# A metaformer block with a spectral filter: combining the spectra at k and -k behind the mixing, scaling in the rectification, and taking the mean of x on TensorE

## Chip, cores and metric

The kernel runs on one core of one Trainium2 chip. The metric is the time of one execution on the device in microseconds (us), as the median of several runs. Lower is better. A change of about 0.5% (14 us) is what a measurement of this kernel can tell from none.

## What is computed

The input x has shape (8, 128, 128, 96): eight images b of 128 x 128 pixels (h, w) with 96 channels. Cut to what matters, the reference is:

```python
z     = layernorm(x)                                  # over the 96 channels
x_pre = scale * relu(z @ w1.T) ** 2 + bias            # 192 channels
xf    = rfft2(x_pre)                                  # over h and w, 128 x 65 frequencies
r     = softmax(mlp([mean(z), mean(relu(bn(z @ sp_w.T)))]))   # 3 weights for each of 192 channels
comb  = sum_s r[s] * resized(cw_s)                    # complex filter, one of three sizes resized to 128 x 65
x     = x + irfft2(xf * comb) @ w2.T
out   = x + ffn_fp8(layernorm(x))                     # 96 -> 384 -> 96, products in float8
```

## The kernel before

Each image passes three streams, which the kernel calls a, s and c.

**Stream a** (function `before`) works in 32 units u of four columns w, and in 8 blocks of 16 columns. `load_x` loads a block with h on the partitions, `measure` takes its statistics on VectorE (DVE), and `rstd` (operations `variance`, `root`, `inverse`, `rest`) turns them into 1/deviation, partly on GpSimd (POOL). `store_r` writes these 128 x 16 numbers to DRAM (`Rd`), and `load_r` reads them back, broadcast over 96 partitions (`rB`, 128 DMAs of 384 KB). `load_xT` loads the same pixels with the channels on the partitions (`zT`, 8 columns at a time, four buffers); a 97th row holds ones, so that the bias of the batch norm comes with the product. `scale` (L771) multiplies `zT` by `rB` on DVE and sums each channel beside it, which gives the mean of z. `project` (L784) multiplies by `w1` and `sp_w` at once (240 columns per image column; the subtraction of the mean is in the weights), `rectify` (L795, ScalarE, ACT) takes two image columns at a time from PSUM through relu, `square` (L802) squares them, and `context` (L809, POOL) adds up the spatial context. `transform` (L813) is the Fourier transform along h, `put` and `fold` combine the halves w and 127-w, and `store_y` writes the result to DRAM. After the last unit nine small steps `rate_v0` to `rate_n` compute the three filter weights.

**Stream s** (function `spectrum`) works on 33 groups g. A group up to 30 holds four rows of the real transform along h, that is cosine and sine at two frequencies k and k+32. `load_y` and `load_t` load them and the filter rows (from `T`, filled at the start by `rows` and `row_put`), `weigh` (L987, POOL) applies the weights, `along_w` (L997) is the transform along w, and `filters_of` (L1014) resizes the filters along w, on 52 of 64 rows, `T` having rows 52 to 63 filled with zeros by `padding`. `copy_sr`, `make` (L1037), and `times` (L1043, L1048) build the spectra at k and -k and multiply them by the filters. `turn_back` (L1059, POOL) forms real and imaginary parts of both products into `rr`, and `real_basis` (L1072, L1074, POOL) adds and subtracts those of k and -k into `xf`. For each of 16 pairs p of groups, `mix_low` and `mix` (L1108) multiply by `w2` on quarters of TensorE (64 x 64, each a product of 96 columns) into two PSUM banks `pv`; `mixed` (L1126, ACT) copies each (384 columns) to `V`, `invert` (L1130) is the inverse transform along w, `inverted` copies it, and `store_v` stores it. The last pair also holds the frequencies 0, 32 and 64, which stand alone.

**Stream c** (function `after`) takes the inverse transform along h (`last`, L1216), adds x, normalises (`measure`, `rstd`, `quantise` L1240), and runs the float8 layers: `turn8`, `first` (L1259), `accumulated` (L1266), `biased` (L1270), `hidden` (L1274), `second` (L1281), `put8`, `bias` (L1296), `add_up` (L1299, POOL), `store`.

**What sets the order.** Nothing runs in the order in which it is written. Each step is an `Op` with the steps that it needs and the PSUM banks it takes (six banks are shared; `until` names what frees one). `in_order` is a list scheduler: it plays through the five engines with a cost for each kind of step (`COST`), picks among the steps that are ready by a place (`WINDOWS` for stream and image, `OFFSETS` for the kind, `WAIT`, `PATIENCE` and `TURN` as weights), and the program is then issued in that order, fixed on every engine. DMAs of SyncE (SP) stand in one such order too; ACT issues `store_y` and `store_v`. Most buffers are two deep, so that a step waits for the step two blocks, groups or pairs earlier.

Of the kernel before, what the change touches and what calls it, by code (L numbers as in the profile page):

```python
# [34 lines left out]
F32 = mybir.dt.float32  # L35
# [33 lines left out]
    "a": ((-493.8, 43.6), (391.2, 548.2), (341.5, 669.9), (360.3, 112.8), (272.4, 474), (949.3, 682.8), (1532.2, 298.2), (2022.4, 291.1)),  # L69
    "s": ((419.4, 108), (361.2, 702.1), (621.3, 470.7), (1129.7, 501.9), (1112.5, 414.1), (1261.5, 485.3), (2142.2, 519.8), (1769.1, 212.4)),  # L70
    "c": ((643.4, 448.3), (913.9, 146.9), (1128.5, 301.3), (1948.4, 242), (1978.4, 471.2), (2323.9, 476.2), (2115.4, 99.6), (2601.6, 522.4)),
}
OFFSETS = {
    "a_context": -48.63,
    "a_fold": 49.78,
    "a_inverse": -197.71,
    "a_load_r": -12.98,
    "a_load_x": 18.54,
    "a_load_xT": -82.99,
    "a_measure": 28.7,  # L80
    "a_project": 54.76,
    "a_put": 22.3,
    "a_rate_e": -72.58,
    "a_rate_n": 307.71,
    "a_rate_p0": -87.61,
    "a_rate_p1": -45.78,
    "a_rate_p2": 8.73,
    "a_rate_v0": -246.94,
    "a_rate_v1": 95.58,
    "a_rate_v2": -255.23,  # L90
    "a_rate_v3": 112.84,
    "a_rectify": 7.95,
    "a_rest": 13.94,
    "a_root": -29.71,
    "a_scale": 65.86,
    "a_square": -3.1,
    "a_store_r": 47.62,
    "a_store_y": -73.43,
    "a_transform": -140.71,
    "a_variance": 57.57,  # L100
    "c_accumulated": -127.17,
    "c_add_up": -24.29,
    "c_bias": -7.57,
    "c_biased": -79.11,
    "c_first": -54.8,
    "c_hidden": 21.22,
    "c_inverse": 24,
    "c_last": -35.87,
    "c_load_v": -86.64,
    "c_measure": 192.55,  # L110
    "c_put8": 71.54,
    "c_quantise": 113.84,
    "c_quantise_v": 412.46,
    "c_residual": 7.8,
    "c_rest": -56.04,
    "c_root": 58.58,
    "c_second": -187.49,
    "c_store": 64.06,
    "c_turn8": -545.98,
    "c_turned8": 70.7,  # L120
    "c_variance": -102.78,
    "s_alone_t": 116.39,
    "s_alone_x": 156.62,
    "s_alone_z": 122.58,
    "s_along_w": -138.44,
    "s_copy_sr": -78.4,
    "s_filters_of": -23.17,
    "s_invert": -43.99,
    "s_inverted": -179.15,
    "s_load_t": 88.39,  # L130
    "s_load_y": 36.3,
    "s_make": 62.83,
    "s_mix": 40.57,
    "s_mix_low": -82.45,
    "s_mixed": -49.42,
    "s_real_basis": 33.95,
    "s_store_v": -18.14,
    "s_times": -182.14,
    "s_turn_back": 123.89,
    "s_weigh": -6.86,  # L140
}
WAIT, PATIENCE, TURN = (0.1, 0, 0, 0.06, 1.5), (16.9, 0.166, 10.6, 0.53, 42.4), 13.18
# [13 lines left out]
    "a_project": (PE, 0.975, 0),  # L156
    "a_transform": (PE, 0.809, 0),
    "a_rectify": (ACT, 0.57, 0),
# [4 lines left out]
    "a_scale": (DVE, 1.215, 0),  # L163
# [3 lines left out]
    "a_rest": (POOL, 1.11, 0),  # L167
# [10 lines left out]
    "s_real_basis": (POOL, 0.91, 0),  # L178
# [3 lines left out]
    "s_mixed": (ACT, 0.48, 0),  # L182
    "s_invert": (PE, 0.81, 0),
# [4 lines left out]
    "c_last": (PE, 0.809, 0),  # L188
# [14 lines left out]
    "a_rate_v0": (DVE, 0.73, 0),  # L203
    "a_rate_p0": (PE, 0.25, 0),
    "a_rate_v1": (DVE, 0.14, 0),
# [6 lines left out]
    "_make_weights": (DVE, 7.4, 0),  # L212
    "_others": (DVE, 1.5, 1),
    "_weights": (DVE, 5, 2),
    "_padding": (POOL, 1, 2),
    "_rows": (PE, 1.2, 0),
    "_row_put": (DVE, 1.25, 1),
    "_next_pool": (SP, 0, 0),
# [271 lines left out]
def metaformer_kernel(ctx: ExitStack, tc: tile.TileContext, a: dict, out: bass.AP):  # L490
# [465 lines left out]
    def spectrum(b, t0, P):  # L956
# [164 lines left out]
        def mix(p):  # L1121
            mix_part(p, (2, 3))
# [297 lines left out]
```

## Time and profile before

| | us |
|---|---|
| median of 3 runs | 2853.39 |
| lowest and highest | 2841.11, 2855.94 |
| the profiled execution | 2853.48 |
| its span in the profile | 2851.7 |
| TensorE (PE) busy | 2493.0 |
| VectorE (DVE) busy | 2273.5 |
| ScalarE (ACT) busy | 2130.2 |
| GpSimd (POOL) busy | 2062.8 |

The mean granted clock of TensorE is 0.933 of full speed, and the DMA engines moved 621.55 MB. In the profile, L12 is line 12 of the kernel; a group of instructions has a line `engine op out<-in`, the shapes, the count, its busy time, the mean of one in ns, and the idle time of its engine ahead of it with what ended it. A float32 product counts as two matmul records. Busy times of a group are those in which at least one of its instructions ran.

### The profile page before, as it was taken

How to read it: one execution, taken by the hardware profiler on the slowest of the kernel's cores; microseconds unless marked ns; L12 is line 12 of the kernel's file. 1: busy time of each engine (PE TensorE's matmuls, PEld its weight loads, DVE VectorE, ACT ScalarE, POOL GpSimd, SP SyncE). 2: the span in 40 equal slices, each digit the busy share in tenths (PEclk: the TensorE clock that was granted, in tenths of full speed). 3: DMA queues.
4: the chain of work that ended last, by engine and by line, in shares of the span. 5: the costliest groups of instructions: out<-in, count | busy, mean ns of one | idle time of the engine just before them, and what ended most of it. 6: DMA issues, size and time to landing. Idle time of an engine off the chain costs nothing. (4 is left out here: it accounts for less than half of the span.)

```text
span 2851.7 us, 98748 instructions
## 1 busy us (share of the span) xinstructions
PE 2493.0 (87%) x40122; PEld 1759.1 (62%) x40122; DVE 2273.5 (80%) x5110; ACT 2130.2 (75%) x4204; POOL 2062.8 (72%) x2983
## 2 busy tenths in 40 slices
PE   5788999899998999988989999999899888887775
PEld 3456666666766676766666666666667555665443
DVE  4567667887997899888878877897888987778785
ACT  2255544688886788978996577779799798787987
POOL 3136886777877887767888788798888787888433
PEclk9689998999999999989999999999999987989876
DMA  7688878988798898977669978785687663666431
GB/s 223 210 280 250 245 208 230 294 234 231 227 277 240 223 275 261 276 230 220 201 181 276 287 223 249 216 258 163 205 242 224 178 188 110 197 178 172 156 122 56
DMA packets 785657, 621.55 MB, mean 218 GB/s; under 512 B 578366, under 2 KB 719558, under 8 KB 785178
## 3 DMA queue, kind: packets, MB, share of 16 engines
q1 hardware_dynamic: 697138, 464.21, 58.9%
q10 hardware_dynamic: 88064, 151.02, 14.9%
q8 instruction: 316, 5.18, 0.8%
q14 instruction: 139, 1.14, 0.1%
HBM read 406.92 MB, written 208.16 MB: 216 GB/s over the span
## 5 line engine op out<-in xcount | busy, mean ns | idle before, releaser
L1059 POOL TENSOR_TENSOR rr<-t 128x390 f32<-128x390 f32 x512 | 500.6, 989 | 145.9 <-DVE t L1043 142.9
L784 PE MATMUL px<-W1S,zT 97*128 97x240 f32 x2048 | 513.8, 390 | 38.6 <-DVE yst L825 15.3
L784 PEld LDWEIGHTS px<-W1S,zT 97*128 97x128 f32 x2048 | 391.1, 199 | 137.9 <-DVE yst L825 23.8
L1266 ACT CAST y<-ph 128x512 f16<-128x512 f32 x768 | 410.9, 603 | 43.8 <-PE ph L1259 38.7
L813 PE MATMUL py<-X,F 128*128 128x384 f32 x1024 | 422.9, 530 | 16.4 <-ACT sr L1030 3.0
L795 ACT ACTIVATE rl<-px 128x480 f32<-128x480 f32 x512 | 289.9, 577 | 168.8 <-PE px L784 142.6
L1240 ACT ACTIVATE z<-t,ln_m,ln_r 128x96 fp8e5<-128x96 f32 x960 | 407.3, 476 | 10.8 <-DMA yt<-Yd 5.0
L1274 ACT ACTIVATE h<-y 128x1536 fp8e5<-128x1536 f16 x256 | 383.9, 1501 | 22.5 <-DVE y L1270 11.7
L1037 DVE TENSOR_TENSOR d<-pz,sr 128x390 f32<-128x390 f32 x512 | 265.7, 553 | 133.8 <-ACT sr L1030 132.6
L1270 DVE TENSOR_TENSOR y<-y,b1q 128x1536 f16<-128x1536 f16 x256 | 317.3, 1240 | 57.2 <-ACT y L1266 55.7
L1108 PE MATMUL pv<-w2C,xf 64*64 64x96 f32 x12288 | 319.9, 251 | 28.7 <-issue 24.0
L825 DVE TENSOR_TENSOR yst<-py,yb 128x384 f32<-128x384 f32 x512 | 261.8, 547 | 98.3 <-ACT yb L819 50.8
L809 POOL TENSOR_TENSOR sacc<-sacc,rl 128x192 f32<-128x192 f32 x248 | 167.7, 676 | 222.4 <-ACT rl L795 214.7
L1108 PEld LDWEIGHTS pv<-w2C,xf 64*64 64x64 f32 x12288 | 283.9, 138 | 71.6 <-issue 46.5
L987 POOL TENSOR_TENSOR tb<-tb,r 128x384 f32<-128x384 f32 (+1 forms) x264 | 302.0, 1145 | 27.2 <-DMA tb<-T 26.4
L1072 POOL TENSOR_TENSOR xf<-rr 128x390 f32<-128x390 f32 x256 | 291.3, 1138 | 13.6
L1043 DVE TENSOR_TENSOR t<-d,pf 128x780 f32<-128x780 f32 x256 | 245.2, 958 | 63.2 <-PE pf L1014 33.4
L1259 PE MATMUL ph<-zT,W1q 96*128 96x512 fp8e5 x768 | 258.4, 420 | 35.5 <-DVE zT L1255 20.0
L997 PEld LDWEIGHTS pz<-F,yt 64*64 64x64 f32 x12480 | 225.6, 138 | 93.6 <-issue 34.3
L997 PE MATMUL pz<-F,yt 64*64 64x65 f32 x12480 | 257.1, 226 | 20.6 <-issue 8.4
L1014 PE MATMUL pf<-RW,tb 52*64 52x130 f32 x6240 | 243.0, 283 | 31.7 <-POOL rr L1059 8.7
L1074 POOL TENSOR_TENSOR xf<-rr 128x378 f32<-128x378 f32 x256 | 266.9, 1043 | 0.0
(117 smaller groups left out, 4509.2 us busy)
## 6 DMA issues: line engine op xcount, KB each, us to landing
yt<-Yd SPq DMA_DIRECT2D x1040, 96.0 KB
Yd<-yst ACTq DMA_DIRECT2D x256, 384.0 KB
xb<-in_xw SPq DMA_DIRECT2D x64, 768.0 KB
zT<-in_xT SPq DMA_DIRECT2D x128, 384.0 KB
rB<-Rd SPq DMA_DIRECT2D x128, 384.0 KB
tb<-T SPq DMA_DIRECT2D x256, 192.0 KB
Vd<-gst ACTq DMA_DIRECT2D x128, 384.0 KB
t<-in_x SPq DMA_DIRECT2D x64, 768.0 KB
```

The costliest lines, as they stand in the source:

```text
L784: nc.tensor.matmul(px[:, i * (MED + SCTX) : (i + 1) * (MED + SCTX)], lhsT=zTs[(b * NU // 2 + u // 2) % NZT][:, QW * (u % 2) + i0 + i, :], ...
L795: nc.scalar.activation(kept["rl", u][:, i0 : i0 + 2, :].rearrange("h w m -> h (w m)"), kept.pop(("px", u, i0)), AF.Relu)
L813: nc.tensor.matmul(py, lhsT=F1, rhs=kept["X", u][:, i0 : i0 + 2, :].rearrange("h w m -> h (w m)"), start=True, stop=True)
L987: nc.gpsimd.tensor_tensor(kept["tb", g][p, :], kept["tb", g][p, :], rates[b][p, :], ALU.mult)
L997: nc.tensor.matmul(halves[i][64 * k : 64 * k + 64, c * L : (c + 1) * L], lhsT=kept["yt", g][rows, cs, q, k, :], rhs=F2[rows, cs, :], start ...
L1059: nc.gpsimd.tensor_tensor(out, t[:, :, 0, :], t[:, :, 1, :], ALU.add if i else ALU.subtract)
L1072: nc.gpsimd.tensor_tensor(xf[:, :, :, 0:L], two(g, 0, 2, 0, L), two(g, 1, 2, 0, L), ALU.add)
L1108: nc.tensor.matmul(kept["pv", p, r][half, i * C : (i + 1) * C], lhsT=kept["xf", g][rows, cs, q, half], rhs=w2C[rows, q, :], start=(i == 0 ...
L1240: nc.scalar.activation(z, t, AF.Identity, bias=m, scale=r, saturate=False)
L1266: nc.scalar.copy(kept["y", u][:, n, :], kept.pop(("ph", u, n)))
L1270: nc.vector.tensor_tensor(y, y, b1q, ALU.add)
L1274: nc.scalar.activation(kept["h8", u], kept["y", u], AF.Relu, saturate=False)
```

## The change

Three things are done, and the order is made anew.

1. *Spectra.* `turn_back` writes real and imaginary parts of the products at k and -k straight into `xf`; `real_basis` and `rr` are gone. `mix` multiplies these by `w2` (and `w2N`, its negative, for one quarter), `mixed` copies only the half of -k from PSUM to `B` (192 columns), and a new step `combine` on DVE forms sum and difference of k and -k, 4 times a pair, reading one operand from PSUM. `invert` uses `GL` for the sums and a second matrix `GM` for the differences. The rows of `GK` are ordered to match. The columns at the two real frequencies of the half transform are now made in the filters (`ends`, `end_put`, twelve more rows of `T`, in place of the zeros), so that `filters_of` contracts over all 64 rows.
2. *1/deviation.* `scale`, `store_r`, `load_r` and `rB` are gone. `project` works on the unscaled `zT`; `rectify` multiplies by 1/deviation as it takes relu, as a per-partition scale, and so one image column at a time. The 97th row of `zT` holds the deviation instead of ones: `rest` computes it with two more small operations on POOL, `store_s` writes it to DRAM transposed (elements of 4 bytes), and `put_s` loads it as one row.
3. *Mean of z.* `gsum` multiplies x by 1/deviation on TensorE, 16 products a block, each of 32 equal columns of weights and 96 columns of x, on four strips of 32 columns of the array; `gadd` adds the blocks on DVE, and `rate_p0` and `rate_v1` finish.

Besides, `load_x` has three buffers instead of two, `invert` and `mix_low` wait for the pair two earlier instead of one, and `WINDOWS`, `OFFSETS`, `WAIT`, `PATIENCE`, `TURN` and some of `COST` have new values. The core of the diff:

```diff
-WAIT, PATIENCE, TURN = (0.1, 0, 0, 0.06, 1.5), (16.9, 0.166, 10.6, 0.53, 42.4), 13.18
+WAIT, PATIENCE, TURN = (0.07, 0.06, 0, 0.09, 2.83), (18.8, 8.11, 4.79, 4.13, 60), 1.3
...
-    "a_rectify": (ACT, 0.57, 0),
+    "a_rectify": (ACT, 0.615, 0),
+    "a_gsum": (PE, 0.9, 0),
+    "a_gadd": (DVE, 0.25, 0),
+    "a_put_s": (SP, 0.48, 0.2),
+    "a_store_s": (SP, 0.55, 2.2),
...
-        def scale(hb):
-            z = zTs[(b * NU // 2 + hb) % NZT][:C, :, :]
-            nc.vector.scalar_tensor_tensor(z, z, 1.0, kept["rB", hb], ALU.mult, ALU.mult,
-                accum_out=kept["gacc"][:, hb : hb + 1])
+        def store_s(blk):
+            t = kept["Sd", blk] = dram.tile([WB, H], F32, name="Sd", tag="Sd")
+            with nc.allow_non_contiguous_dma("deviations by columns"):
+                nc.sync.dma_start(out=t.rearrange("w h -> h w"), in_=kept["sd", blk])
+        def put_s(hb):
+            z = zTs[(b * NU // 2 + hb) % NZT][C : C + 1, :, :]
+            f = slice((hb % 2) * HB, (hb % 2) * HB + HB)
+            nc.sync.dma_start(out=z.rearrange("o w h -> o (w h)"),
+                in_=kept["Sd", hb // 2][f, :].rearrange("(o w) h -> o (w h)", o=1))
+        def gsum(blk):
+            pc = kept["pc", blk] = bank("pc")[:, :C]
+            for i in range(QW):
+                for j in range(4):
+                    w = QW * j + i
+                    nc.tensor.matmul(pc[32 * j : 32 * j + 32, :],
+                        lhsT=kept["r", blk][:, w : w + 1].to_broadcast([128, 32]),
+                        rhs=kept["x", blk][:, w, :], start=(i == 0), stop=(i == QW - 1))
...
-            nc.scalar.activation(
-                kept["rl", u][:, i0 : i0 + 2, :].rearrange("h w m -> h (w m)"), kept.pop(("px", u, i0)), AF.Relu
-            )
+            for i in range(2):
+                w = q * QW + i0 + i
+                nc.scalar.activation(kept["rl", u][:, i0 + i, :],
+                    px[:, i * (MED + SCTX) : (i + 1) * (MED + SCTX)], AF.Relu,
+                    scale=kept["r", blk][:, w : w + 1])
...
-                        p = slice(64 * s, 64 * s + R)
+                        p = slice(64 * s, 64 * s + 64)
...
+            x = kept["xf", g].rearrange("p s q n -> p (s q) n")
             if i == 0:
                 t = kept["t1", g].rearrange("p s (q c l) -> p (s q) c l", q=3, c=2)
+                nc.gpsimd.tensor_tensor(x[:, :, 0:L], t[:, :, 0, :], t[:, :, 1, :], ALU.subtract)
             else:
-                t = kept["t2", g]
-            out = kept["rr", g][:, 2 * i : 2 * i + 2].rearrange("p s q l -> p (s q) l")
-            nc.gpsimd.tensor_tensor(out, t[:, :, 0, :], t[:, :, 1, :], ALU.add if i else ALU.subtract)
-        def real_basis(g, i):
-            if i == 0:
-                nc.gpsimd.tensor_tensor(xf[:, :, :, 0:L], two(g, 0, 2, 0, L), two(g, 1, 2, 0, L), ALU.add)
-            else:
-                nc.gpsimd.tensor_tensor(xf[:, :, :, L:], two(g, 2, -1, 1, L - 2), two(g, 3, -3, 1, L - 2), ALU.subtract)
+                t = kept["t2", g][:, :, :, 1 : L - 1]
+                nc.gpsimd.tensor_tensor(x[:, :, L:], t[:, :, 0, :], t[:, :, 1, :], ALU.add)
...
         def mixed(p, r):
-            v = kept["V", p, r] = psp.tile([128, 4 * C], F32, name="V", tag="V")
-            nc.scalar.copy(v, kept.pop(("pv", p, r))[:, : 4 * C])
+            v = kept["B", p, r] = psp.tile([128, 2 * C], F32, name="B", tag=f"B{r}")
+            n = C if p == NP - 1 and r == 1 else 2 * C
+            nc.scalar.copy(v[:, :n], kept["pv", p, r][:, 2 * C : 2 * C + n])
+        def combine(p, r, cs):
+            v, a, b = kept["V", p, cs][:, r, :n], kept["pv", p, r][:, :n], kept["B", p, r][:, :n]
+            if cs == 0:
+                nc.vector.tensor_tensor(v, a, b, ALU.add)
+            else:
+                nc.vector.tensor_tensor(v, b, a, ALU.subtract)
+        def invert(p, cs):
+            pg = kept["pg", p, cs] = bank("pg")[:, : 4 * C]
+            nc.tensor.matmul(pg[:, :n], lhsT=GM if cs else GL, rhs=v[:, :n], start=True, stop=True)
...
-            at(t, mix_low, p, after=xf, banks=2, until=[one("mixed", p, r) for r in range(2)])
+            used = [[one("mixed", p, r), one("combine", p, r, 0), one("combine", p, r, 1)] for r in range(2)]
+            at(t, mix_low, p, after=xf, banks=2, until=used)
```

## Prediction

> **What bounds the kernel now.** I read the busy times first, then the same times by stage, then who TensorE waits for, then the groups that the change touches.
>
> ```profile
> PE 2493.0 (87%) x40122; PEld 1759.1 (62%) x40122; DVE 2273.5 (80%) x5110; ACT 2130.2 (75%) x4204; POOL 2062.8 (72%) x2983
> ```
>
> TensorE (PE) is the fullest, but only on average. The busy times by stretch (window, length, then PE, PEld, DVE, ACT, POOL) split at three events: the first spectral matmul (about 230 us), the last projection `px` (2204) and the last spectral matmul (2661):
>
> ```profile
> 0.00:230.00 230.00, 165.88 (x531) 107.01 (x532) 129.74 (x464) 92.33 (x167) 68.94 (x200) 0.84 0.76 237
> 230.00:2204.00 1974.00, 1821.09 (x31068) 1312.58 (x31067) 1630.33 (x3600) 1500.48 (x2985) 1558.02 (x2191) 0.97 0.82 237
> 2204.00:2661.00 457.00, 381.12 (x7707) 265.72 (x7706) 374.50 (x727) 375.61 (x766) 374.60 (x480) 0.91 0.59 169
> 2661.00:2851.00 190.00, 124.90 (x821) 73.76 (x821) 138.97 (x321) 161.75 (x288) 61.27 (x114) 0.69 0.34 111
> ```
>
> In the long stretch, 69% of the span, PE is busy 92%, and DVE (83%), POOL (79%) and ACT (76%) follow it. Only the last 190 us belong to ACT (85%). PE idles 64 + 153 + 76 + 65 = 358 us in all. The waits of PE within the long stretch (us in total, times, longest) are many and small; summed over that list by releaser they are ACT 65.8, no visible cause ("issue") 38.0, DVE 21.3, POOL 16.2, DMA 5.4:
>
> ```profile
> PE pv L1108 <- issue: 21.4, 15, 4.2
> PE pf L1014 <- POOL rr L1059: 8.3, 6, 3.6
> PE px L784 <- ACT sr L1030: 5.1, 3, 4.2
> ```
>
> So POOL, from which the change takes most, delays PE by some 16 us there; ACT delays it four times as much. The groups that the change touches, each shape apart (busy us, mean ns of one, then idle before it):
>
> ```profile
> L1059 POOL TENSOR_TENSOR rr<-t 128x390 f32<-128x390 f32 x512 | 500.6, 989 | 145.9 <-DVE t L1043 142.9 <-DVE t L1048 2.5
> L1240 ACT ACTIVATE z<-t,ln_m,ln_r 128x96 fp8e5<-128x96 f32 x960 | 407.3, 476 | 10.8 <-DMA yt<-Yd 5.0 <-POOL ln_m L729 2.5 <-DVE t L1048 1.5
> L1072 POOL TENSOR_TENSOR xf<-rr 128x390 f32<-128x390 f32 x256 | 291.3, 1138 | 13.6
> L795 ACT ACTIVATE rl<-px 128x480 f32<-128x480 f32 x512 | 289.9, 577 | 168.8 <-PE px L784 142.6 <-PE pz L997 3.6 <-DMA Yd<-yst 3.2
> L1074 POOL TENSOR_TENSOR xf<-rr 128x378 f32<-128x378 f32 x256 | 266.9, 1043 | 0.0
> L771 DVE SCALAR_TENSOR_TENSOR zT<-zT,rB 96x1024 f32<-96x1024 f32 x128 | 191.5, 1496 | 23.4 <-DMA zT<-in_xT 17.3 <-DMA rB<-Rd 3.8 <-DMA Rd<-ln_r 2.2
> L1126 ACT COPY V<-pv 128x384 f32<-128x384 f32 x256 | 111.9, 486 | 125.2 <-PE pv L1108 119.1 <-DMA yt<-Yd 2.9 <-PE py L813 2.4
> ```
>
> **What the skill says.** (1) "ScalarE: Activation LUTs", section "What ACT_TABLE_LOAD costs": an activation with immediate scale and bias takes 186 ns + 0.833 ns an element, each per-partition operand adds about 93 ns, neighbours overlap by about 93 ns. The trace agrees: by it L795 (480 wide, no such operand) is 586 ns, measured 577; L1240 (96 wide, two of them) is 452, measured 476. (2) "TensorEngine Tiling (Array Packing)", sections "Available Configurations" and "Key Properties": 128x32 gives four independent tiles, and a change of tiling mode drains the array. The trace has no 128x32 tile; it shows the drain (below). (3) "DMA: Bandwidth & Descriptors", "Rules for kernel authors": a last dimension that isn't contiguous becomes one descriptor per element. No run here shows that yet.
>
> **The change part by part**, against the profiled execution: 2853.48 us, of which the span is 2851.7, and 1.8 lie around it. The median of the runs, 2853.39, is the same.
>
> *POOL.* `real_basis` goes: 291.3 + 266.9 = 558 us. `turn_back` stays at 512 instructions, now written in the layout of `xf`: between L1059's 989 ns and the mean of L1072 and L1074 (1090), so 0 to +52; I take +30. `rest` gets two 128x16 operations for each of 64 blocks, 128 x 284 ns (L728, L729: 286 and 281) = +36. POOL falls by about 490, to 55% of the span. What it can give the end is what PE waits for it: 16 us, and some 5 more through DVE (its `y` addition, L1270, has a mean of 1240 ns against a median of 984, which I read as collisions with POOL).
>
> *DVE.* `scale` goes: 191.5, its accumulator reads 9.8, and the reduction of `gacc` 2.4: -204. `combine` adds 8 x 16 x 4 = 512 additions of 192 columns from PSUM. Nearest row: L913, a 192-wide copy from PSUM, 345 ns: +177 (bounds 262 and 519 ns, the 192-wide rows L928 and L915: 134 to 266). `gadd` adds 64 of 96 columns at some 250: +16. Net -11, from -54 to +78; DVE isn't the bound, so I count 0.
>
> *ACT.* `rectify` becomes 1024 activations of 240 columns with one per-partition scale: by (1) 479 ns each. Three `y` copies in a row take 1.60 us in the timeline where 3 x 603 are 1.81, an overlap of 0.1 each. Before 512 x (577 - 100) = 244, after 1024 x (479 - 100) = 388: +144 (+20 if the operand's 93 ns and some more hide, +195 if nothing overlaps). The kernel's own planner has 0.615 us for a pair, against 0.57 for the single one, so the new order allows for little of this. `mixed` halves to 192 columns: 256 x 486 = 124 becomes, by (1), 248 x 346 plus 24 of 96 columns at 266, 92: -32. Net ACT +112, all of it ahead of the last projection, where ACT goes from 76% to some 80%. PE's 66 us of waits for ACT grow in proportion at least (112 / 1500 of 66 = 5), and faster as slack goes: I take +10, range 5 to 30.
>
> *PE.* `gsum` adds 64 x 16 matmuls of 96 columns on 128x32 tiles. Nearest row: the mixing `pv`, also 96 columns in f32, four quarters side by side. In the chain of waits:
>
> ```profile
> 2190.23 2.01 PE pv L1108 x96
> ```
>
> That is 96 records or 48 matmuls, 12 rounds of four, 0.168 us a round. Four rounds for a block: 0.67, and 0.13 for entering and leaving: 0.8 x 64 = +51. Below: 43, if it joins a run of quarters. Above: if the four tiles don't run side by side, 16 x 0.168 x 64 = +172. Against that the new order changes less often between whole and divided array: counted in the two programs' PE order, 876 times before and 636 after. The price of one, in the PE timeline (start, length):
>
> ```profile
> 1242.06 1.52 PE L813 MATMUL py<-X,F 128*128 128x384 f32 x4
> 1243.42 0.81 PE L1216 MATMUL pk<-vin,GK 128*128 128x384 f32 x2
> 1244.16 0.93 PE L997 MATMUL pz<-F,yt 64*64 64x65 f32 x48
> 1245.02 0.42 PE L1245 MATMUL pz<-ident,z 128*96 128x128 fp8e5 x4
> ```
>
> `pk` starts 0.16 us ahead of the end of `py` (same mode), `pz` 0.07 ahead of the end of `pk`, and the next again 0.07: a change costs 0.09. 240 x 0.09 = -22. `ends` adds 12 matmuls at about 0.75 (L639's rows): +9; the split last inversion +2. The longer contraction of `filters_of` (52 to 64 rows) costs nothing, its columns being the same. Net PE +40 (32 to 160).
>
> *PSUM.* The two `pv` banks of a pair are now held until the copy and two `combine` on DVE are through, 0.35 + 2 x 0.35 instead of 0.49, plus DVE's queue; six banks serve everything. `invert` waits for all of it. Two pairs may be in flight instead of one, which covers most: +6, range 0 to 20.
>
> *DMA and SP.* 128 broadcasts of 384 KB go (50 MB of 621). The store of 8 KB a block becomes 2048 elements of 4 bytes: 131,072 packets more. Queue q1 took 58.9% for 697138 packets: 38.5 ns of one engine each, at 666 B on average. At that price they take 131072 / 16 x 38.5 ns = 315 us of all 16 engines, and 50 MB at q10's rate (151 MB in 14.9%, 355 GB/s) give back 142. Lower bound: packets for nothing. So the share of 75% moves by -5 to +6 points, from 82 to at most 91 in the long stretch: no bound. SP issues as many (64 + 128 for 64 + 128); the single `put_s` row waits behind `store_s` on it, with the loads of `yt` behind both. `project` loses the wait for a 1.5 us `scale` and gets one for a later store; the three `xb` buffers cover that. I count 0, above +40.
>
> Sum: 2853.5 + 40 - 16 - 5 + 10 + 6 = 2888; I say **2888**, 1.2% slower. The parts' own range: 2865 to 2915.
>
> **Rivals.**
> 1. *Faster: PE's idle time shrinks by more than PE's work grows.* All hinges on the 153 us of scattered idle in the long stretch: with POOL at 55% and 240 fewer changes of mode the fixed order may stall PE less. At 4% idle instead of 7.7: PE 2533, idle 65 + 80 + 141, around it 2: 2821; and the new order leaves less for the ACT-bound end (summing rows after the last `px`: ACT 599 us before, 444 after), worth up to 35: 2786. Middle 2805. It decides once idle falls from 358 below 318. For it: no single wait is large. Against: the largest releaser, ACT, gets more work.
> 2. *The array's 128x32 tiles run one after another:* 172 for 51, so 3009. The tiling page speaks against it.
> 3. *ACT or DMA takes over:* rectification at its upper bound and 4-byte packets at their price or above; PE's idle grows by 40 more: 2930. For it: nobody's price in this trace covers 4-byte runs. Against: ACT stays near 80%.
>
> **Numbers.** Forecast 0.48, rival 1 0.28, rival 2 0.04, rival 3 0.20. Within 0.5% (2839 to 2868, about what a measurement of this kernel can tell from no change) lie 0.10 of the forecast's and 0.04 of rival 1's chance. Faster 0.24, same 0.14, slower 0.62. The range reaches from rival 1's middle to beyond rival 3: 2805 to 2950; the forecast's own is 2865 to 2915.
>
> **What would show it.** Right: PE busy near 2533, ACT near 2240, POOL near 1570, DVE within 80 of before; `gsum` near 0.8 us a block; `rl` near 480 ns; idle of PE still 340 to 370, with ACT its first releaser. Wrong: PE idle under 318 (rival 1); `gsum` near 2.7 us (rival 2); DMA share over 90% with waits for `zT` or `Sd` (rival 3).

## Result, and the profile after

| | before | after |
|---|---|---|
| median of 3 runs, us | 2853.39 | 3331.29 |
| lowest and highest | 2841.11, 2855.94 | 3330.18, 3342.53 |
| span of the profiled execution | 2851.7 | 3340.7 |
| mean granted clock of TensorE | 0.933 | 0.881 |

The changed kernel takes 1.17 times as long, 95% interval 1.1635 to 1.1765. The forecast was 2888 and the range ended at 2950: neither held. The page of the changed kernel, busy times and DMA queues:

```profile
PE 2689.0 (80%) x42226; PEld 1944.4 (58%) x42226; DVE 2190.9 (66%) x5429; ACT 2211.4 (66%) x4732; POOL 1458.6 (44%) x2594
DMA packets 894834, 572.14 MB, mean 171 GB/s; under 512 B 699508, under 2 KB 840876, under 8 KB 894336
...
q1 hardware_dynamic: 806296, 414.51, 51.0%
q10 hardware_dynamic: 88064, 151.02, 18.3%
```

No engine is fuller than before. PE works 196 us longer and idles 652 us instead of 358. Queue q10 (the stores that ACT issues) carries exactly the packets of before, but they take 18.3% of 3340.7 = 611 us instead of 14.9% of 2851.7 = 425. The stretches, split at the same events (first spectral matmul, last `px`, last spectral matmul; then PE, PEld, DVE, ACT, POOL, clock, DMA share, GB/s):

```profile
0.00:270.00 270.00, 188.32 (x852) 118.88 (x856) 94.29 (x348) 101.77 (x222) 48.11 (x167) 0.81 0.75 142
270.00:2845.00 2575.00, 2124.83 (x35228) 1567.37 (x35220) 1710.87 (x4216) 1711.37 (x3729) 1177.00 (x2075) 0.90 0.74 180
2845.00:3156.00 311.00, 260.92 (x5388) 187.93 (x5386) 258.96 (x551) 246.88 (x511) 174.42 (x249) 0.90 0.56 163
3156.00:3340.70 184.70, 114.93 (x772) 70.23 (x772) 126.75 (x314) 151.34 (x272) 59.08 (x106) 0.69 0.33 109
```

All the loss lies ahead of the last `px`, where stream a runs: 2845 us instead of 2204, of which 146 come back in the third stretch because work of streams s and c has moved forward. The last two columns of the long stretch matter most: the DMA share fell (0.82 to 0.74), and so did what was moved (237 to 180 GB/s). The share says how long packets are under way, not how much arrives. The groups that the change touches:

```profile
L848 ACT ACTIVATE rl<-px,ln_r 128x240 f32<-128x240 f32 x1024 | 412.9, 480 | 247.4 <-PE px L833 151.2 <-DMA zT<-in_xT 16.8 <-DMA yt<-Yd 13.0
L1114 POOL TENSOR_TENSOR xf<-t 128x390 f32<-128x390 f32 x256 | 230.9, 902 | 626.0 <-DVE t L1100 604.8 <-PE pv L1152 14.5 <-PE ph L1332 5.6
L1185 DVE TENSOR_TENSOR V<-pv,B 128x192 f32<-128x192 f32 x248 | 87.2, 352 | 145.6 <-ACT B L1171 130.3 <-ACT V L1177 11.3 <-PE ph L1332 3.7
L1171 ACT COPY B<-pv 128x192 f32<-128x192 f32 x248 | 69.2, 329 | 205.4 <-PE pv L1152 163.1 <-remote 30.5 <-PE pz L1318 7.2
L814 PE MATMUL pc<-xb,ln_r 128*32 128x96 f32 x2048 | 76.5, 279 | 86.0 <-issue 53.8 <-POOL ln_r L556 16.8 <-ACT y L1339 9.1
```

Each operation costs about what was expected of it (furthest off is `gsum`, `pc`, with 76.5 us for 51). The time is in between them. PE's waits by releaser went from ACT 154, no visible cause 43, DVE 83, POOL 32, DMA 27 to ACT 230, no visible cause 256, DVE 70, POOL 34, DMA 40. ACT in turn waits 184 us where a DMA ended last (before: 54). On SP's own queue two waits of the new steps stand out (us in total, times, longest):

```profile
SPq L807 <- DMA Sd<-ln_s: 222.8, 38, 13.9
SPq L802 <- POOL ln_s L769: 145.8, 41, 9.8
```

L802 is `store_s`, L807 is `put_s`: the row waits for the store of 8 KB, and does so for up to 13.9 us. One such store, as the timeline shows it (start, length):

```profile
1267.88 0.38 SPq L802 DMA_DIRECT2D Sd<-ln_s  x1
...
1268.30 1.13 SPq L1035 DMA_DIRECT2D tb<-T  x1
...
1271.12 1.02 DVE L881 TENSOR_TENSOR yst<-py,yb 128x384 f32<-128x384 f32 x2 [2.07 <-PE py L869]
...
1272.20 1.08 PE L833 MATMUL px<-W1S,zT 97*128 97x240 f32 x4 [0.29 <-DVE yst L881]
...
1279.91 0.25 SPq L807 DMA_DIRECT2D zT<-Sd  x1
...
1280.71 0.52 ACTq L885 DMA_DIRECT2D Yd<-yst  x1
1281.35 0.81 ACT L848 ACTIVATE rl<-px,ln_r 128x240 f32<-128x240 f32 x2 [7.69 <-DMA tb<-T]
1282.22 1.97 PE L833 MATMUL px<-W1S,zT 97*128 97x240 f32 x4 [7.24 <-ACT rl L848]
```

and what the engines do meanwhile, in steps of 2 us (columns as above):

```profile
1266.00:1268.00 2.00, 0.63 (x32) 0.44 (x24) 2.00 (x8) 1.17 (x4) 1.66 (x6) 1.00 0.88 223
1268.00:1270.00 2.00, 1.40 (x16) 0.66 (x16) 1.05 (x7) 1.20 (x4) 2.00 (x3) 1.00 0.49 16
1270.00:1272.00 2.00, 1.74 (x26) 0.95 (x26) 0.88 (x2) 2.00 (x3) 1.29 (x2) 1.00 0.14 1
1272.00:1274.00 2.00, 1.63 (x6) 1.02 (x7) 2.00 (x10) 1.66 (x5) 0.96 (x5) 1.00 0.42 35
1274.00:1276.00 2.00, 0.98 (x4) 0.33 (x2) 1.37 (x3) 0.00 (x0) 0.86 (x2) 1.00 0.43 30
1276.00:1278.00 2.00, 0.00 (x0) 0.00 (x0) 0.00 (x0) 0.00 (x0) 0.00 (x0) 1.00 0.25 34
1278.00:1280.00 2.00, 0.00 (x0) 0.00 (x0) 0.00 (x0) 0.00 (x0) 0.00 (x0) 0.57 0.15 32
1280.00:1282.00 2.00, 0.00 (x0) 0.00 (x0) 0.00 (x0) 0.65 (x2) 0.99 (x1) 0.50 0.83 190
1282.00:1284.00 2.00, 1.78 (x5) 1.35 (x6) 1.08 (x3) 1.98 (x5) 0.00 (x0) 0.50 1.07 382
```

Once the store is issued, all transfers together fall from 223 GB/s to between 1 and 35 for 12 us. ACT stands in front of its own store of `yst`, whose data were ready at 1272.14, until 1280.71; `rl` waits behind it on ACT, `px` for `rl`, and from 1276 to 1280 every engine is idle. What the store of `yst` waits for is a semaphore: the DMAs of SP and ACT count their landings on eight that they share, and the issue of this one stands until the load of `tb`, issued at 1268.30 on the same semaphore, has landed at 1280.68. Such waits of ACT ahead of its stores are 234 us in this kernel and 70 in the kernel before.

This is no unlucky spot: averaged over the 64 stores, the rates of the table further down show the same hole. The single packets and landings in the trace say two things more. The store's own packets don't fill the hole: in the median of the 64 stores, 95% of the 4-byte packets have started 2.6 us after the issue, and one is under way for some 10 ns. And other transfers land late, on both queues: a load of `yt` issued in the 6 us behind a store takes 11.5 us to land (median; 4.4 over all loads of `yt`), a store of `yst` 12.4 (4.9).

### The profile page after: what moved, and what is told of

Same layout as the page of the kernel before. It is cut to its first block, busy times and chain, and to the rows that moved or that the text cites. A ratio compares the mean times of both kernels' runs of the same rounds, so it can differ in the third digit from the quotient of the medians.

```text
span 3340.7 us, 103404 instructions
## 1 busy us (share of the span) xinstructions
PE 2689.0 (80%) x42226; PEld 1944.4 (58%) x42226; DVE 2190.9 (66%) x5429; ACT 2211.4 (66%) x4732; POOL 1458.6 (44%) x2594
## 3 DMA queue, kind: packets, MB, share of 16 engines
q10 hardware_dynamic: 88064, 151.02, 18.3%
## 5 line engine op out<-in xcount | busy, mean ns | idle before, releaser
L848 ACT ACTIVATE rl<-px,ln_r 128x240 f32<-128x240 f32 x1024 | 412.9, 480 | 247.4 <-PE px L833 151.2
L1114 POOL TENSOR_TENSOR xf<-t 128x390 f32<-128x390 f32 x256 | 230.9, 902 | 626.0 <-DVE t L1100 604.8
L1152 PE MATMUL pv<-w2C,xf 64*64 64x96 f32 x9264 | 363.6, 262 | 64.5 <-issue 51.1
L1152 PEld LDWEIGHTS pv<-w2C,xf 64*64 64x64 f32 x9264 | 320.7, 146 | 95.3 <-issue 70.9
L1054 PE MATMUL pz<-F,yt 64*64 64x65 f32 x12480 | 290.9, 231 | 96.8 <-issue 77.7
L1054 PEld LDWEIGHTS pz<-F,yt 64*64 64x64 f32 x12480 | 255.2, 143 | 144.2 <-issue 101.0
L1343 DVE TENSOR_TENSOR y<-y,b1q 128x1536 f16<-128x1536 f16 x256 | 277.7, 1085 | 71.7 <-ACT y L1339 70.6
L1071 PE MATMUL pf<-RW,tb 64*64 64x130 f32 x6240 | 264.6, 294 | 43.8 <-issue 16.5
L1332 PE MATMUL ph<-zT,W1q 96*128 96x512 fp8e5 x768 | 252.5, 412 | 39.4 <-DVE zT L1328 13.9
L869 PEld LDWEIGHTS py<-X,F 128*128 128x128 f32 x1024 | 197.2, 207 | 142.5 <-issue 26.6
L1354 PE MATMUL po<-W2q,h 128*128 128x96 fp8e5 x3072 | 193.9, 219 | 101.9 <-ACT h L1347 63.6
```

Of the source, the lines that this page charges most:

```text
L848: nc.scalar.activation(kept["rl", u][:, i0 + i, :], px[:, i * (MED + SCTX) : (i + 1) * (MED + SCTX)], AF.Relu, scale=kept["r", blk][:, w : ...
L869: nc.tensor.matmul(py, lhsT=F1, rhs=kept["X", u][:, i0 : i0 + 2, :].rearrange("h w m -> h (w m)"), start=True, stop=True)
L1054: nc.tensor.matmul(halves[i][64 * k : 64 * k + 64, c * L : (c + 1) * L], lhsT=kept["yt", g][rows, cs, q, k, :], rhs=F2[rows, cs, :], start ...
L1152: nc.tensor.matmul(kept["pv", p, r][half, i * C : (i + 1) * C], lhsT=kept["xf", g][rows, k, q, half], rhs=(w2N if k == 1 and h == 1 else w ...
L1332: nc.tensor.matmul(kept["ph", u, n], lhsT=W1q[:, n * 128 : (n + 1) * 128], rhs=kept["zT", u], start=True, stop=True)
L1343: nc.vector.tensor_tensor(y, y, b1q, ALU.add)
```

## Experiments

The theory after this reading: the store of 2048 elements of 4 bytes holds up every transfer in flight for some 8 us, 64 times. Against it stood: SP's wait for that store (a queue with `yt`, `tb` and the rows behind it); the new engine work, as forecast; and the new order. Every kernel is compared with the kernel before on the same chip; the medians of that one lie between 2840 and 2853 us, so that differences in us between kernels of different chips are good to some 10 us. The diffs are cut to what matters. Unless said otherwise the instructions of each engine stand in the order of the kernel that was edited.

**1. No row at all (e1), and the parts of the change without it (e3, e4).**

```diff
+for t in zTs: nc.gpsimd.memset(t[C : C + 1, :, :], 1.0)
-nc.sync.dma_start(out=t.rearrange("w h -> h w"), in_=kept["sd", blk])                 # store_s
-nc.sync.dma_start(out=z.rearrange("o w h -> o (w h)"), in_=kept["Sd", hb // 2][f, :]...)  # put_s
```

> The changed kernel in its own order on every engine, without the deviation row: neither the store of the deviations to DRAM (64 stores of 2048 elements of 4 bytes) nor the load of the row (128); the 97th row of zT holds ones, as before the change. It leaves out the deviation in the bias of the batch norm. Theory A (the store of 4-byte elements is late and slow, and everything that SyncE's queue holds behind it comes late): the excess of some 440 us over the forecast goes, 2840 to 2910 us, and the wait of SyncE for Sd with it. Rival B (the new order is bad because the rectification, the combine step and the PSUM banks cost more than the planner had): it stays above 3150.

Measured: 2825.69, ratio 0.9921 (0.9901 to 0.9941). All of the 505 us between this and the changed kernel are the store and its row, and without them the change is a little faster than before. e3 is e1 with the old `rectify`:

```diff
-for i in range(2): nc.scalar.activation(rl[:, i0 + i, :], px[...], AF.Relu, scale=kept["r", blk][:, w : w + 1])
+nc.scalar.activation(rl[:, i0 : i0 + 2, :], px, AF.Relu)
```

> As the run without the row, and the rectification as before the change: 512 activations of 480 columns without a scale, instead of 1024 of 240 with one. It leaves out the factor 1/deviation. By the prediction's sum ACT loses 144 us of work and PE some 10 to 30 us of waits: 10 to 40 us below the run without the row. If the rectification is what the planner mis-priced with effect (rival B): 80 or more below.

Measured: 2790.88, ratio 0.9815 (0.9767 to 0.9863), 35 us below e1. e4 is e1 without `gsum` and `gadd`:

```diff
-for i in range(QW):
-    for j in range(4): nc.tensor.matmul(pc[32 * j : 32 * j + 32, :], ...)
-nc.vector.tensor_tensor(kept["gacc"], pc, kept["gacc"], ALU.add)
+nc.vector.memset(kept["gacc"], 0.0)
```

> As the run without the row, and without the mean of z on TensorE: no gsum products and no addition of blocks. It leaves out the mean. By the prediction's sum, 51 us (0.8 us a block) below the run without the row; from 20 (if what it leaves is taken by other waits) to 80 (its measured busy time of 76 us).

Measured: 2781.43, ratio 0.9782 (0.9731 to 0.9833), 44 us below e1. The busy times of e1, the group of `gsum`, its queues, and its stretches (split at the same events again):

```profile
PE 2483.5 (88%) x42226; PEld 1817.2 (64%) x42226; DVE 2185.6 (77%) x5429; ACT 2202.0 (78%) x4732; POOL 1474.1 (52%) x2598
...
L812 PE MATMUL pc<-xb,ln_r 128*32 128x96 f32 x2048 | 58.9, 255 | 36.8 <-POOL ln_r L556 23.6 <-issue 8.0 <-ACT X L856 2.0
...
q1 hardware_dynamic: 673944, 413.46, 52.0%
q10 hardware_dynamic: 88064, 151.02, 14.9%
```

```profile
0.00:191.00 191.00, 160.82 (x810) 103.20 (x811) 89.24 (x337) 95.06 (x213) 49.34 (x163) 0.88 0.64 196
191.00:2343.00 2152.00, 1955.45 (x35258) 1461.82 (x35257) 1713.98 (x4229) 1709.04 (x3738) 1191.17 (x2082) 0.97 0.73 215
```

With the same 42226 matmuls, PE is busy 206 us less than in the changed kernel and idles 343 us instead of 652. So two fifths of the 505 us are PE being busy for longer, and most of that is its clock: the granted clock is 0.97 here in the long stretch, 0.90 there, and in the steps above it drops to 0.57 and 0.50 while the engines stand idle. The same matmuls at a lower clock count as longer busy. By the mean clocks of the two profiles, 2483.5 x 0.942 / 0.881 = 2655 us, an estimate, 172 of the 206 us are the clock's. q10 is back at 14.9%.

**2. The same bytes in runs of 64 bytes (e2).** The wait of SP and the row stay, the transposition goes.

```diff
-nc.sync.dma_start(out=t.rearrange("w h -> h w"), in_=kept["sd", blk])
+nc.sync.dma_start(out=t.rearrange("w (p f) -> (w p) f", f=WB), in_=kept["sd", blk])
```

> The changed kernel with one edit: the deviations are stored in runs of 16 neighbours (128 packets of 64 bytes a block instead of 2048 of 4 bytes); the load of the row, its wait for the store and all orders stay. It leaves the values of the row in another sequence. Theory A1 (the 4-byte elements are the cost): 2850 to 2930 us, within 40 of the run without the row. Theory A2 (any round trip through DRAM with SyncE's queue standing behind it costs the time): above 3100, and SyncE still waits over 150 us for Sd. Rival B: no change, 3330.

Measured: 2848.44, ratio 1.0006 (0.9984 to 1.0027). The way through DRAM with its wait costs 23 us, the 4-byte form of the store the other 483. A store of e2 in steps of 2 us (issued at 1017.76):

```profile
1015.00:1017.00 2.00, 1.50 (x75) 1.31 (x64) 2.00 (x4) 2.00 (x4) 1.75 (x5) 1.00 1.07 297
1017.00:1019.00 2.00, 0.46 (x14) 0.36 (x14) 1.93 (x13) 0.04 (x1) 1.83 (x5) 1.00 0.31 66
1019.00:1021.00 2.00, 1.43 (x8) 0.64 (x4) 0.00 (x0) 1.77 (x5) 2.00 (x3) 0.66 0.76 178
1021.00:1023.00 2.00, 2.00 (x18) 0.93 (x21) 0.65 (x2) 1.65 (x2) 0.18 (x1) 0.50 0.64 137
1023.00:1025.00 2.00, 2.00 (x19) 1.54 (x12) 2.00 (x10) 1.62 (x5) 0.81 (x4) 0.50 0.95 347
```

Here the rate is at 178 GB/s in the step after next.

**3. The wait against the transfers (e5, e8).** e5 keeps the 4-byte store, but takes the row of `zT` from x, so that the row doesn't wait for the store:

```diff
-in_=kept["Sd", hb // 2][f, :].rearrange("(o w) h -> o (w h)", o=1)
+in_=x[b, 0, 0:16, :].rearrange("w c -> (w c)")[0 : HB * H].rearrange("(o n) -> o n", o=1)
```

> The changed kernel with its 4-byte stores in place, but the row of zT is loaded from x in DRAM and not from what was stored: no load waits for a store to land. It leaves out the deviation in the bias of the batch norm. Theory A-wait (SyncE's queue stands until the store has landed, some 13 us a block, and the loads behind come late): 2860 to 2950. Theory A-load (131072 small writes occupy the DMA engines and hold up all other transfers, those of ACT's queue too, whose share of engine time rose from 14.9% to 18.3%): above 3150.

Measured: 3277.97, ratio 1.1536 (1.1505 to 1.1566): only 53 us less. SP's waits for the store are about halved, from 272 to 145 us; they aren't gone, since later DMAs use the store's semaphore. e8 is the kernel before, with a 4-byte store of 1/deviation a block that nobody reads:

```diff
+t = dram.tile([WB, H], F32, name="Sx", tag="Sx")
+nc.sync.dma_start(out=t.rearrange("w h -> h w"), in_=kept["r", blk])
```

> The kernel before, with one addition: beside its store of 1/deviation, each block stores the same 128 x 16 numbers transposed, in 4-byte elements, to a place that nobody reads. Orders are those of before. Theory A-load: the addition alone makes the old kernel slower by 200 to 500 us. Theory A-wait: nobody waits for it, so by 0 to 60 us.

Measured: 3278.65, ratio 1.1528 (1.1498 to 1.1558). One DMA statement does to the old kernel, with its old order, nearly all that the whole change did: 438 us of 478. SP waits only 67 us for that store. So SP's wait is not the main cause, nor is the order. One of its stores, issued at 1252.13:

```profile
1250.00:1252.00 2.00, 2.00 (x95) 1.87 (x92) 2.00 (x5) 0.68 (x2) 2.00 (x5) 1.00 0.95 279
...
1254.00:1256.00 2.00, 2.00 (x38) 1.76 (x31) 2.00 (x4) 0.71 (x3) 2.00 (x3) 1.00 0.38 6
1256.00:1258.00 2.00, 2.00 (x8) 1.34 (x8) 2.00 (x4) 1.53 (x3) 1.73 (x3) 1.00 0.26 4
...
1260.00:1262.00 2.00, 0.66 (x23) 0.53 (x26) 0.00 (x0) 0.00 (x0) 0.00 (x0) 1.00 0.63 39
```

It isn't quite without a wait for the store: the buffer of 1/deviation comes free only when the store has read it, and ACT's square root waits for that:

```profile
ACT ln_r L715 <- DMA Sx<-ln_r: 159.5, 25, 13.0
```

How much of the 438 us comes this way, and how much through the other transfers, e8 does not tell apart. That the others are held up shows here too: a load of `yt` issued in the 6 us behind a store lands after 10.6 us (median; 4.6 over all).

**4. Number or placement of the elements (e6, e11, e18, e13, e9).** e6 stores half of the elements, and both rows come from that half:

```diff
-nc.sync.dma_start(out=t.rearrange("w h -> h w"), in_=kept["sd", blk])
+nc.sync.dma_start(out=t[0:HB, :].rearrange("w h -> h w"), in_=kept["sd", blk][:, 0:HB])
```

> The changed kernel with half of the 4-byte elements: each store writes 8 of 16 columns (1024 elements), and both row loads read that half. It leaves out the other half of the deviations. If the cost goes with the number of elements from the 64-byte version (2848) to the changed kernel (3331): 3030 to 3150. If it is a latency that hardly depends on the number: above 3200. If it has a threshold (covered by the three-deep buffers below some 8 us): under 2950.

Measured: 3240.3, ratio 1.1398 (1.1369 to 1.1427). Half the elements keep 82% of the excess over e1 (415 of 505): the cost is not proportional to them. The other four are e5 with 2048 elements of 4 bytes, set apart in DRAM, the 16 of a partition next to each other (D = 2, 8, 16 or 128 elements of 4 bytes):

```diff
-t = dram.tile([WB, H], F32)
-nc.sync.dma_start(out=t.rearrange("w h -> h w"), in_=kept["sd", blk])
+t = dram.tile([H, WB, D], F32)
+nc.sync.dma_start(out=t[:, :, 0:1], in_=kept["sd", blk].unsqueeze(2))
```

> As the run in which the stored deviations are not read (3278 us), but the 2048 elements of a store lie 512 bytes apart in DRAM, so that no two of them share a stretch of 512 bytes. It leaves out the deviation in the bias of the batch norm. Theory L (writes of 4 bytes that share a stretch of DRAM with writes of other DMA engines wait for one another, and hold up the rest): 2830 to 2900 us, and the transfer rate stays near 220 GB/s after a store. Theory S (any 2048 writes of 4 bytes do it, wherever they go): 3150 or more, and the rate falls to some 50 GB/s for 8 to 10 us.

> As the run before this one, with the elements 8 bytes apart and the 16 of a partition next to one another: a stretch of 512 bytes holds the elements of four partitions only. It leaves out the deviation in the bias of the batch norm. Theory L with stretches of 512 bytes: between the run with 512 bytes and the unread one, 2900 to 3250. Theory L with stretches of 128 bytes or fewer, or if elements of one partition go out through one DMA engine and don't wait for one another: 2830 to 2900. Theory S: 3150 or more.

> As the unread run with elements 512 bytes apart (2912 us), now 64 bytes apart, the 16 of a partition next to one another: 8 elements share a stretch of 512 bytes, none a stretch of 64. It leaves out the deviation in the bias of the batch norm. If sharing a stretch of 64 bytes or less is what hurts: 2880 to 2950. If sharing a stretch of 512 bytes is enough: 3150 or more, as with 8 bytes.

> As the runs with the deviations' elements set apart (the row of zT is loaded from x in its place, so the bias of the batch norm is wrong; nobody reads the store), with 32 bytes from element to element. 64 bytes apart gave 2941, 8 bytes apart 3349. Theory A (what costs is that several 4-byte writes fall into one stretch of 64 bytes): two still share one, so 3150 to 3350. Rival B (the stretch is 32 bytes or less): 2920 to 2970. Rival C (the cost falls steadily with the distance, no edge): 3000 to 3150.

| distance of neighbours | us | ratio to before (95%) | above e1 |
|---|---|---|---|
| 4 bytes, transposed (e5) | 3277.97 | 1.1536 (1.1505 to 1.1566) | 452 |
| 8 bytes (e11) | 3349.41 | 1.1731 (1.1669 to 1.1793) | 524 |
| 32 bytes (e18) | 3060.38 | 1.0744 (1.0689 to 1.0799) | 235 |
| 64 bytes (e13) | 2941.18 | 1.0348 (1.033 to 1.0367) | 115 |
| 512 bytes (e9) | 2911.68 | 1.0201 (1.0145 to 1.0256) | 86 |

The five runs stand on four chips; by the ratios, the last column would be 459, 516, 234, 121 and 80. The number of packets and of bytes is the same in all five, and the 4-byte packets start as fast: in e9, too, 95% have started 2.6 us after the issue. So what makes four fifths of the cost is neither the number of small packets nor the transposition (in e11 a partition's 16 elements are neighbours), but that they lie close together in DRAM. There is no sharp edge: the excess falls from 8 to 64 bytes and little beyond. The transfer rate in GB/s in steps of 2 us from 4 us ahead of the store's issue, averaged over the 64 stores, shows the hole shrink with it:

```
after         216 221 150  62  32  40  39  54 184 278 276
e8            247 243 240 121  28  53  57 118 220 262 240
e6 (half)     197 217 159  74  47  44  47 135 282 280 228
e9 (512 B)    215 224 150  94 151 244 274 259 217 219 223
e14           218 203 191  54  28  44  42  96 275 300 256
e2 (64 B run) 219 215 162 216 220 234 246 214 233 233 232
before        261 266 267 252 236 241 233 258 234 229 235
```

The last line is the store of 1/deviation of the kernel before, whose runs are 64 bytes too; e14 comes in the next experiment. In the changed kernel the hole is about five steps long. With half the elements it is one step shorter.

**5. By which way it reaches the engines (e14, e15, e17).** e14 is the changed kernel, with the stores of Y and V issued by SP:

```diff
-nc.scalar.dma_start(out=Y[b][:, :, 2 * u : 2 * u + 2, :], in_=...)
+nc.sync.dma_start(out=Y[b][:, :, 2 * u : 2 * u + 2, :], in_=...)
```

> The changed kernel with the stores of Y and V issued by SyncE instead of ACT, at the same places of the order; the 4-byte stores stay. If the slow transfers reach the other engines above all through ACT, which can't go on with its arithmetic while the issue of a store stands (ACT, DVE, PE and POOL all idle from 1275 to 1280 us in the trace): under 3150. If they reach them through late loads: 3250 or more.

Measured: 3145.02, ratio 1.1066 (1.1027 to 1.1106), 186 us less. ACT's waits where a DMA ended last fall from 184 us to 1. But the hole is still there (the line of e14 above), and shows elsewhere: POOL waits 254 us for loads of `tb` (109 in the changed kernel), and `yst` on DVE now waits for its buffers.

```profile
L881 DVE TENSOR_TENSOR yst<-py,yb 128x384 f32<-128x384 f32 x512 | 261.4, 547 | 207.0 <-DMA Yd<-yst 97.9 <-ACT yb L875 62.7 <-PE py L869 33.2
```

Two controls, with the same two edits: e15 on e2 (no 4-byte store), e17 on the kernel before.

> The control to the run before this one: stores of Y and V on SyncE, deviations in runs of 64 bytes (128 packets a block); it leaves the values of the row in another sequence. 2830 to 2890, as with the stores on ACT (2848).

> The kernel before with the same two edits as control. Theory (the gain has nothing to do with the change): 2760 to 2810. Rival (in the kernel before, ScalarE has slack enough where it stores, and SyncE's queue with 128 broadcasts more holds the stores up): 2835 to 2870.

Measured: e15 2774.32, ratio 0.9771 (0.9745 to 0.9798), 74 us less than e2, which was not expected; e17 2777.57, ratio 0.9769 (0.9724 to 0.9814), some 71 less than before. So of the 186 us some 74 have nothing to do with the change; the other 112 go with the waits of ACT in front of its stores for earlier DMAs on the same semaphore, of which e14 has none left. With the stores on SP the 4-byte form still costs 3145 - 2774 = 371 us: most of the hole reaches the engines through late loads and full store buffers.

**6. A version without the fault (e7, e12, e16), and one part alone (e10).** In e7 TensorE turns the deviations by one product with the identity, and 16 rows of 512 bytes are stored:

```diff
-nc.sync.dma_start(out=t.rearrange("w h -> h w"), in_=kept["sd", blk])
+nc.tensor.matmul(pb[:WB, 128:256], lhsT=kept["sd", blk], rhs=ident, start=True, stop=True)
+nc.vector.tensor_copy(sT, pb[:WB, 128:256])
+nc.sync.dma_start(out=t, in_=sT)
```

> A mended change that computes everything: the 128 x 16 deviations of a block are turned on TensorE by one more product with an identity, into the bank of gsum, copied on DVE, and stored as 16 rows of 512 bytes; the load of the row stays. The order is made anew with the planner's costs of these steps. With the 4-byte elements as the only cause: 2820 to 2870, as the version with 64-byte runs, and some 25 us of DVE and 15 us of PE more work than that. If any wait of SyncE for a round trip through DRAM costs: above 2900.

Measured: 2890.18, ratio 1.0162 (1.0123 to 1.02), missed by 20 us. Its order is made anew, but with windows and offsets found for another program; that this is the reason was not tested by itself. e12 is e7 with a truer cost of `rectify` and `WINDOWS`, `OFFSETS`, `WAIT`, `PATIENCE`, `TURN` searched anew:

```diff
-"a_rectify": (ACT, 0.615, 0),
+"a_rectify": (ACT, 0.82, 0),
```

> The mended change (deviations turned on TensorE, stored as rows of 512 bytes; everything computed), with 0.82 us for a pair of rectifications in the planner's costs, and windows, offsets and weights searched anew against the planner. By the ratio of planner to chip of the kernel before (2629 to 2847): 2800 to 2850 us, 0 to 1.6% faster than before. If an order from a search is no better on the chip than the one of the first mended version: 2870 to 2900.

Measured: 2843.36, ratio 0.9967 (0.9945 to 0.9988): without the fault, and with a new search, the change is worth 10 us, less than the 14 that count as a change. e10 is the kernel before with part 1 of the change alone (spectra), searched anew in the same way:

```diff
-nc.scalar.copy(v, kept.pop(("pv", p, r))[:, : 4 * C])
+nc.scalar.copy(v[:, :n], kept["pv", p, r][:, 2 * C : 2 * C + n])
+nc.vector.tensor_tensor(V[:, r, :n], kept["pv", p, r][:, :n], kept["B", p, r][:, :n], ALU.add if cs == 0 else ALU.subtract)
```

> Part 1 of the change alone: spectra at k and -k combined behind the mixing; the scaling by 1/deviation on DVE and the mean from it stay as before the change. Everything is computed. Windows, offsets and weights searched anew against the planner, as long as for the mended version. It gives POOL's 520 us back and costs DVE 177 us, without the rectification's and gsum's work: by the runs without these two (35 and 44 us) less what scale costs DVE (204 us, not the bound): 2770 to 2840. If POOL's work was of no account and the DVE work counts: 2850 or more.

Measured: 2904.71, ratio 1.018 (1.0135 to 1.0225), a miss. DVE keeps `scale` and gets `combine`:

```profile
PE 2463.3 (85%) x40162; PEld 1791.9 (62%) x40162; DVE 2331.7 (80%) x5629; ACT 2103.3 (72%) x4220; POOL 1507.7 (52%) x2470
```

POOL is relieved by 555 us, PE is busy less than before, and the time still grows. Whether that is DVE's load or a search that stopped too soon was not told apart. Last, e16 is e12 with its stores on SP.

> The version with the deviations turned by TensorE and the order searched anew (2843), with the stores of Y and V issued by SyncE instead of ScalarE; the computation is complete. Theory (a store costs ScalarE time whatever the shape of the deviations' store, as the row of 64-byte runs showed with 74 us): 2755 to 2800. Rival (those 74 us belonged to ScalarE waiting behind the deviations' store of 128 packets, which is gone here in favour of 16 rows of 512 B): 2825 to 2850.

Measured: 2797.97, ratio 0.9848 (0.9805 to 0.9892). It beats both kernels, but the control e17, on the same chip, lies at 0.9769: the change adds nothing to that edit. e15 gives up the transposition and so is no rival of e17.

## Why the prediction was wrong

The step that failed is **DMA and SP**: "So the share of 75% moves by -5 to +6 points, from 82 to at most 91 in the long stretch: no bound. ... I count 0, above +40." What it counted as 0 cost 483 to 505 us (e2, e1), and the store alone cost 438 in the kernel before (e8). Three things in it have to be told apart.

- *The price of a packet was not too low.* 0.510 x 3340.7 - 0.520 x 2826.4 = 234 us of 16 engines for 132,352 packets more in q1 than in e1 (131,072 of the stores, 1280 of the row). Only some 80 of them are the 4-byte packets themselves, at 10 ns of one engine each, where the step used 38.5; the other 154 are packets that e1 has too and that take longer here. The section "Rules for kernel authors" of the Trainium skill's page "DMA: Bandwidth & Descriptors", which says that such a store becomes one descriptor per element, is borne out by the counts.
- *The kind of cost was wrong.* The step treated a transfer as work that fills free engine time, and so found room under 100%. What the store does is hold up all others, for some 10 us at 30 to 60 GB/s. A share of busy time can't show this: it fell by 8 points in the long stretch while the kernel lost 478 us. "Rival 3" had the right suspect (nobody's price in the trace covered 4-byte runs), but the first half of its sign, "DMA share over 90%", would have cleared it; only the second half, "waits for `zT` or `Sd`", came.
- *The upper end was no bound.* No working stands behind the "+40", and the rate per packet came from packets of 666 bytes on average, with no store made of 4-byte elements among them. The wait of `put_s` behind `store_s` was seen, but taken to be short; it was 222.8 us over 38 times. Yet with the row's wait gone the kernel is only 53 us faster (e5).

The other steps, read from e1, where this one is taken out:

- *POOL*: -490 forecast, to about 1570; 1474 in e1. `turn_back` became faster (901 and 954 ns instead of 989), where +30 was allowed for. That it gives little by itself, as forecast, fits e10, where POOL is relieved and the kernel no faster; it was not tested without the other parts of the change.
- *DVE*: 2185.6 against 2273.5, -88, just outside "within 80"; `combine` at 351 ns against 345. DVE is no bound here; whether it is one when `scale` stays, e10 leaves open.
- *ACT*: `rl` 484 ns (480 in the changed kernel) where the page "ScalarE: Activation LUTs", section "What ACT_TABLE_LOAD costs", gave 479; ACT 2202 against near 2240. The step allowed +10 for the waits; the whole rectification costs 35 us (e3), just above the range of 5 to 30. `mixed` at 332 ns against 346.
- *gsum*: 58.9 / 64 = 0.92 us a block for 0.8, 44 us in the run (e4, without `gadd` too) for 51. The four tiles do run side by side, as "TensorEngine Tiling (Array Packing)" has it; rival 2 (2.7 us) falls.
- *PE +40*: PE is busy 2483.5 in e1, 10 us less than before, though `gsum` alone adds 59. `px` falls from 513.8 to 484.9 and `py` from 422.9 to 400.4 with the same instructions. e1's granted clock is 0.942 against 0.933, and 2483.5 x 0.942 / 0.933 = 2507: some 24 of the 50 us that PE stays under the forecast of 2533 are the clock's, by this estimate, and the rest is not explained. That the clock moves the busy time had no place in the sum.
- *Idle time of PE*: 343 in e1 against 358; the forecast's 340 to 370 holds.

So without the store the change would have come to -21 on the same chip (e1) where the parts' sum gives +35: a miss of 2%, on the side of rival 1, but not by its way (idle below 318). Which of the terms makes it (clock, 50 MB fewer broadcasts at the start, fewer changes of mode) was not told apart.

What stays open: why 4-byte writes close together hold up the other transfers. The runs show that distance in DRAM decides, that it falls gradually up to 64 bytes, and that some 60 us of the 2048 packets remain at 512 bytes (1.0201 against e2's 1.0006). What happens inside the memory or the DMA engines, no view shows.

## What to carry to other kernels

A DRAM store whose elements lie 4 bytes apart and are written one by one is not a matter of its 8 KB, nor of its packets times their price: check whether it stops the others, by the GB/s in steps of 2 us around its issue, before trusting a free share of DMA time. Turn the data on an engine first (e12), or write whole runs (64 bytes were enough here, e2); a turned load of what was written in such runs was not tried. And count DMA issue as work of the engine that issues: it isn't in the busy time, it stands in the engine's order, and ahead of it may stand a wait for an earlier DMA, of another engine too, on the same semaphore.

## What the runs showed of the hardware

- One 4-byte store of 2048 neighbouring elements takes all transfers from some 220 to 30 to 60 GB/s for about 10 us, though 95% of its own packets have started after 2.6; set 64 bytes apart, three quarters of the loss is gone, and at 512 bytes four fifths (115 and 86 of 452 us).
- ACT's 256 stores of Y at 0.521 us and 128 of V at 0.326 are 175 us in its queue that no busy time counts. Moving them to SP gave 71 us to the kernel before (e17), 74 to e2 (e15), and 45 to e12 (e16; 34 by the ratios, the two being on different chips). How much of this is the issue itself and how much ACT's waits ahead of it (70 us in the kernel before) was not told apart.
- The granted clock of TensorE fell to 0.5 at 1278.3, 3.3 us after the last matmul ahead of the idle stretch, and the matmuls after it take nearly twice as long: `px`, 4 records, 1.97 us at 1282.22, against 1.08 at 1272.20. The other engines need not stand still for this: in e2 it fell at 1019.6, after a pause of PE of 2.0 us in which DVE and POOL worked. It falls 102 times in the changed kernel's profile and 51 times in e1's. A hole in the transfers is paid a second time in this way, some 172 of 505 us here by the estimate from e1.
